# Conditioned residual block: tiles in pairs that share a matrix, norm products by seven half products

## The chip, the cores and the metric

One core of a Trainium2 chip runs the whole kernel. The metric is the device time of one execution in microseconds; 924.09 us is the median of three runs of the kernel before (919.81 to 926.35). The engines are TensorE (PE, with its weight loads shown as PEld), VectorE (DVE), ScalarE (ACT), GpSimd (POOL) and SyncE (SP, which issues DMA).

## The reference

x is 16 x 512 tokens of 512 floats. Every token has a pathway id (0 to 499), a compartment id c (0 to 4, used for cp and tm) and a flag m (0 or 1, an index into three rows of ms). All is fp32.

```python
h = _ln(x, pw_g[pathway_ids], pw_b[pathway_ids])
h = _ln(h, cp_g[compartment_ids], cp_b[compartment_ids])
t = _ln(x, tm_g[time_steps], tm_b[time_steps])          # time_steps is the same c
m = x + _mlp_ln(memory_state, ...)[:, None, :]           # n and r alike, one row per batch
s = _ln(x, ms_g[scale_type], ms_b[scale_type])           # scale_type is m
cat = concatenate([w[0]*h, w[1]*t, w[2]*m, w[3]*n, w[4]*r, w[5]*s], axis=-1)
return x + _ln(silu(cat @ int_W1 + int_b1) @ int_W2 + int_b2, int_g, int_be)
```

With xn the normalised x, `cat @ int_W1` is x times one fixed matrix (X), the twice normalised h times a fixed matrix (H), xn times a matrix that depends on the token's group (c, m) alone (V), and a row that depends on batch and group.

## The kernel before

**Head.** The 8192 tokens are sorted by their group (15 groups of c and m). Each token's place comes from running counts (`of_grp`, `run`, `pc`, `pos`). `one_hots` then makes, eight columns of tokens at a time, a one-hot of the row within a tile (`rows_`) and one of the tile (`cols_`, times the token's number): VectorE makes five or six of the eight `cols_` by a comparison and a multiplication over all of them, ScalarE the others; TensorE multiplies both into `pn`, the sorted list. Small GpSimd steps find where groups end (`place_borders`, `count_rows`, `segments`, `segment_kinds`, `segment_picks`). A tile of 128 tokens uses the matrix of the group of its middle token; tokens of another group in it get a correction from eight extra tiles, whose results go to `rows_2` in DRAM and are gathered as the row `add` (`ga`). Besides, the head computes the conditioning rows and the weights.

**Windows.** 64 tiles are worked in 16 windows of four (Q = 4). `PLACES` sets which: window w has tiles 2w and 2w+1 of the first half of the sorted order (places g = 0 and 2) and of the second half (g = 1 and 3). Per tile: gather x, statistics and norm (ScalarE), the h branch (VectorE, ScalarE, GpSimd), three turns on VectorE and DMAs on SP's queue (`spread_row`) that bring X, V and H into `cats`, the products of layer 1 in PSUM, adding of `add`, silu, a turn and DMAs into Z, layer 2, norm, output by an indirect DMA.

**Products.** X and H of a pair of tiles (2p, 2p+1) are a 2 x 2 block product done by seven half products instead of eight (`half_product`, `m7`, 4 calls of 128x256 each), with token sums on VectorE (`token_sum`, u1 to u4) and partial sums in the PSUM tiles `u` and `p1`; `half_out` (r1, r2, r3, r5) adds the parts of `u` to `add`. r1 adds the first product, while `u` holds it alone. V is done whole, four calls of 128x512 per tile (`layer1` with blk V, line 404). Its matrix is in `vs[g % 2]`, one buffer per half of the order, and is built anew only where the group changes (`s_part` on ScalarE line 257, `build` on VectorE line 265, both under `if_new`). Layer 2 is by seven too (`z_sums` on GpSimd, `seventh`, line 546), but whole in the last window (`layer2`, line 487). Window 0 uses whole products for all three blocks (lines 404).

**Order.** Every engine works its instructions in the order of the program. That order is written out by hand as names: `ORDER` (head and start), `WINDOW` (run for each w from 0 to 14, with p, c, n, m for the previous, this, the next and the window after) and `LAST`. PSUM has eight tiles of 128x512, taken in turn by `psum`.

Of the kernel before, what the change touches and what calls it, by code (L numbers as in the profile page):

```python
# [15 lines left out]
P = 128  # L16
# [10 lines left out]
    gx.e0.2 gc.0.2 fs.0.2 bd.0.1 hv.0.0 tk.1 wk.2.3 fv.0.2 gx.e0.3 cr xs.e0.1 xs.e0.2 xs.e0.3 rp.0 lX.0.1 vt.0.0
    rp.1 f2.0.2 xa.0 xe.e0 gr.e0.1 gh.0.1 fp.0.2 gx.e1.0 gx.e1.3 gx.e1.1 gx.e1.2 gr.e0.0 xp.e0 cw xm.e0 rc.0
    vv.0.1 rc.1 vv.0.3 nv.e0.1 mt.e0.1 vd.0 nv.e0.0 sp.0.0 fn.0.2 nv.e0.2 mt.e0.0 f1.0.1 lX.0.2 fs.0.1 bd.0.0
    fv.0.1 ey.1 ey.0 xs.e1.1 ro.1 ro.0 rp1 vv.0.0 xs.e1.0 xs.e1.2 ez.0 nv.e0.3 ez.1 wh gc.0.1 gr.e0.2 gx.1.2 ea.0  # L30
    lX.0.0 rp2 wl.4 xs.e1.3 f2.0.1 va.1 xs.1.2 gx.1.3 tx.1.2 xe.e1 xs.1.3 ht.0.2 ex.0 ee.0 mt.e0.2 gr.e0.3 gx.1.0
    gh.0.3 fp.0.1 lV.0.0 ey.2 eo.0 gr.e1.0 gx.1.1 xp.e1 fn.0.1 va.0 ez.2 ar mt.e0.3 hv.0.2 xa.1 tx.1.0 vd.1 xm.e1
    tx.1.3 ey.3 ht.0.1 ea.1 gc.0.3 ea.2 gh.1.3 xs.1.0 sp.0.2 ez.3 nv.e1.2 nv.e1.0 ex.1 ex.2 f1.0.3 bd.0.2 fs.0.3
    fv.0.3 mt.e1.0 ex.3 ey.4 f2.0.3 wb xs.1.1 wm.0 wm.1 wm.2 ea.3 fp.0.3 gr.e1.2 gr.e1.1 mt.e1.2 xe.1 hv.0.1 ey.6
    fn.0.3 ez.4 nv.e1.1 wm.3 nv.e1.3 ea.4 xp.1 gr.e1.3 ee.1 tx.1.1 ee.2 mt.e1.1 mt.e1.3 f1.1.3 xm.1 ee.3 eo.2 eo.1
    eo.3 ht.0.3 ey.5 ex.4 lV.0.1 ey.7 lV.0.2 ez.6 wl.2 ez.5 wl.0 ez.7 nv.1.1 nv.1.0 sp.0.3 fs.1.3 gh.1.2 sh.0.0
    gc.1.3 hv.0.3 tv.1.1 tv.1.0 bd.0.3 f1.1.2 fv.1.3 f2.1.3 ex.7 lX.0.3 lV.0.3 lH.0.2 lH.0.3 ex.6 lH.0.1 ex.5
    lH.0.0 ea.6 gc.1.2 ea.5 fp.1.3 ea.7 nv.1.3 sp.1.0 fs.1.2 fn.1.3 nv.1.2 sp.1.1 bd.1.0 tv.1.3 fv.1.2 ee.6 ee.5
    ee.4 th.1.3 f2.1.2 bd.1.1 tv.1.2 ee.7 sX.1.0 eo.4 eo.5 eo.6 eo.7 sV.1.1 sX.1.3 sV.1.0 sX.1.1 sV.1.3 sX.1.2
    sV.1.2 gc.1.0 sh.0.1 gh.1.1 fp.1.2 gh.1.0 sh.0.2 ga.0.3 sh.1.2 ga.0.1 ga.0.0 gc.1.1 ga.0.2 fn.1.2 wl.3 th.1.2  # L40
    wz f1.1.0 f1.1.1 ha.0.3 ha.0.1 ha.0.0 fs.1.0 fs.1.1 hs.0.1 hs.0.0 hs.0.3 wl.1 fv.1.0 f2.1.0 fv.1.1 tz.0.1
    tz.0.0 f2.1.1 ha.0.2 tz.0.3 sh.1.3 gx.2.0 fp.1.0 sh.1.0 gx.2.2 sh.0.3 fp.1.1 hs.0.2 fn.1.0 fn.1.1 tz.0.2 wq
    th.1.1 th.1.0 sZ.0.0 sZ.0.1 sZ.0.2 sZ.0.3 gx.2.1 gx.2.3 sH.1.3 sH.1.2 sH.1.1 sh.1.1 sH.1.0
# [28 lines left out]
    m7.c.0.4 m7.c.0.3 q7.p.1.5 q7.p.1.7 q7.p.1.1 r3.c.1 ha.c.2 ft.p.0 r3.c.0 ft.p.1 ha.c.3 ha.c.1 ha.c.0 hs.c.3
    hs.c.2 hs.c.1 hs.c.0 kf.p.2 kf.p.3 tz.c.3 tz.c.1 e0 tz.c.0 tz.c.2 sf.p.3 w2 po.p.1 sh.c.3 zs.p.7 po.p.0 sZ.c.0
    q7.p.1.6 q7.p.1.4 q7.p.1.2 q7.p.1.3 l2.c.0 ku.p.1 sl.p.2 sl.p.3 sf.p.2 yg.p.3 yg.p.2 la.c.0 lq.p.3 lq.p.2
    sd.p.3 sd.p.2 lq.c.0 sd.c.0 sZ.c.2 sZ.c.1 sZ.c.3 rv.p.2 rv.p.3 ft.p.2 rv.c.0 ft.p.3 yg.c.0 ft.c.0 l2.c.2
    l2.c.1 l2.c.3 po.p.2 po.p.3 po.c.0 la.c.2 la.c.1 lq.c.1 sd.c.1 lq.c.2 sd.c.2 rv.c.1 yg.c.1 ft.c.1 la.c.3
    yg.c.2 yg.c.3 rv.c.2 ft.c.2 e1 lq.c.3 sd.c.3 po.c.1 rv.c.3 ft.c.3 po.c.2 po.c.3
"""


@with_exitstack
def kernel(ctx: ExitStack, tc: tile.TileContext, a: dict, out: bass.AP):

# [26 lines left out]
    Q = 4  # L113
# [1435 lines left out]
```

## Time and profile before

| | us |
|---|---|
| median of 3 runs | 924.09 |
| lowest, highest | 919.81, 926.35 |
| span of the profiled execution | 920.3 |
| busy in it: PE, DVE, POOL, ACT | 884.8, 733.6, 666.9, 521.2 |

The span runs from the first to the last instruction of one profiled execution; the median lies 3.8 us above it. A group of a line is "engine operation, out<-in, shape, count | busy, mean ns of one | idle before it and what ended that". Matmuls are pipelined and their ends are modelled, so the time that a product costs in a stream is read from the start of one to the start of the next, not from its mean. Each fp32 matmul of the program is two instructions in the trace.

### The profile page before, as it was taken

To read this page: it belongs to the slowest core of one execution; us is meant where nothing else is said; L and a number is where in the kernel's file an instruction comes from. 1 tells how busy PE (TensorE), PEld (TensorE's weight loads), DVE (VectorE), ACT (ScalarE), POOL (GpSimd) and SP (SyncE) were. 2 spreads that over 40 slices of the span, in tenths; PEclk is the share of its full clock that TensorE was granted. 3 is DMA by queue.
4 is the path that set the end of the run, shared out by engine and by line. 5 is a ranking of instruction groups with operands and counts; after the bars stand their busy time and mean duration, and the time that the engine had idled before them with its cause. 6 is when DMAs were issued, how large, how long until landed. Compare 5 with 4: busy or idle time off the path is not lost.

```text
span 920.3 us, 13563 instructions
## 1 busy us (share of the span) xinstructions
PE 884.8 (96%) x3617; PEld 642.0 (70%) x3617; DVE 733.6 (80%) x1360; ACT 521.2 (57%) x1263; POOL 666.9 (72%) x730
## 2 busy tenths in 40 slices
PE   6979899999999999999999999999999999999996
PEld 6634446868677777868686877777686867778682
DVE  8776767878789798978787887869697888879565
ACT  5568736464555738374646556473657566572413
POOL 9876678576768678686878686877767676876452
PEclk9999999999999999999999999999999999999999
DMA  8755677777767777777777777777667776776513
GB/s 272 249 185 179 220 226 197 207 210 204 235 178 232 202 218 195 215 208 202 227 202 227 187 235 191 226 193 216 186 197 210 203 220 191 221 200 190 154 37 113
DMA packets 88557, 185.40 MB, mean 201 GB/s; under 512 B 24324, under 2 KB 24388, under 8 KB 88476
## 3 DMA queue, kind: packets, MB, share of 16 engines
q0 software_dynamic: 31104, 104.88, 39.4%
q1 hardware_dynamic: 56668, 79.53, 29.6%
q8 instruction: 30, 0.49, 0.2%
q14 instruction: 51, 0.42, 0.2%
q10 hardware_dynamic: 704, 0.08, 0.1%
HBM read 100.48 MB, written 19.97 MB: 131 GB/s over the span
## 4 chain that ended last, share of the span: by engine, by line
PE 50%; POOL 5%; DVE 4%; issue 3%; DMA 3%; SPq 2%; ACT 1%; POOLq 0%; DVEq 0%; ACTq 0%
PE u L452 13%; PE p L404 13%; PE p L452 11%; PE pq_0b L546 4%; PE pq_1b L546 4%; PE pq_1a L546 3%; PE pq_0a L546 2%; SPq L205 2%; DMA catZ<-rZ 2%; POOL xbs L391 1%; POOL out L638 1%; DMA pw<-in_pw,i_pw 1%; DVE vs L265 1%; DVE yb L634 0%; DVE yb L633 0%
## 5 line engine op out<-in xcount | busy, mean ns | idle before, releaser
L404 PE MATMUL p<-vs,catV 128*128 128x512 f32 x512 | 228.3, 593 | 3.9 <-DVE vs L265 1.7
L404 PEld LDWEIGHTS p<-vs,catV 128*128 128x128 f32 x512 | 96.9, 190 | 108.5 <-issue 99.6
L452 PE MATMUL p<-wh__81,catH 128*128 128x256 f32 x480 | 111.0, 379 | 0.0
L452 PEld LDWEIGHTS p<-wh__81,catH 128*128 128x128 f32 x480 | 91.4, 190 | 12.2
L376 ACT ACTIVATE pw<-pw,rsh 128x512 f32<-128x512 f32 x64 | 45.6, 714 | 95.2 <-DVE pw L383 76.9
L638 POOL DMA_INDIRECT out<-yb,tok x64 | 75.4, 1178 | 31.2 <-issue 15.1
L475 ACT ACTIVATE add<-add 128x512 f32<-128x512 f32 x64 | 39.7, 625 | 94.4 <-DVE add L472 93.1
L350 ACT ACTIVATE junk<-pw 128x512 bf16<-128x512 f32 x60 | 37.5, 626 | 85.8 <-DVE pw L347 78.1
L171 POOL DMA_INDIRECT cp<-cp_rows,i_cp x64 | 73.4, 1147 | 15.5 <-issue 13.2
L391 POOL TENSOR_TENSOR xbs<-xbs,rows 128x512 f32<-128x512 f32 x64 | 82.4, 1289 | 1.4
L171 POOL DMA_INDIRECT pw<-in_pw,i_pw x64 | 63.0, 984 | 28.1 <-DVE rH L197 13.0
L625 POOL TENSOR_TENSOR rsy<-vey,mhalf 128x4 f32<-128x4 f32 (+1 forms) x16 | 23.6, 1473 | 82.3 <-DVE veh L368 69.5
L171 POOL DMA_INDIRECT xbs<-in_x,tok x64 | 65.1, 1017 | 19.9 <-issue 18.1
L171 POOL DMA_INDIRECT add<-rows,i_add x64 | 67.0, 1048 | 16.6 <-issue 16.5
L383 DVE SCALAR_TENSOR_TENSOR pw<-pw,sumsh,cp 128x512 f32<-128x512 f32 x60 | 45.5, 760 | 32.9 <-DMA cp<-cp_rows,i_cp 32.8
L317 ACT ACTIVATE xm<-xbs,nmx,rsx 128x512 f32<-128x512 f32 x64 | 48.8, 806 | 22.9 <-DVE nmx L311 17.2
L372 POOL TENSOR_TENSOR rsh<-veh,mhalf 128x1 f32<-128x1 f32 x64 | 48.6, 760 | 13.0 <-DVE veh L368 11.5
L347 DVE SCALAR_TENSOR_TENSOR pw<-pw,rsx 128x512 f32<-128x512 f32 x64 | 56.0, 876 | 2.3
L452 PE MATMUL p<-wt,catH 128*128 128x256 f32 x240 | 56.7, 379 | 0.0
L452 PE MATMUL u<-wt,catX 128*128 128x256 f32 x240 | 56.5, 379 | 0.0
L452 PEld LDWEIGHTS u<-wx__80,catX 128*128 128x128 f32 x240 | 45.7, 190 | 12.6 <-issue 3.8
L452 PE MATMUL u<-wt,ss 128*128 128x256 f32 x240 | 54.4, 379 | 0.0
(439 smaller groups left out, 2127.7 us busy)
## 6 DMA issues: line engine op xcount, KB each, us to landing
catX<-rX SPq DMA_DIRECT2D x240, 64.0 KB
catV<-rV SPq DMA_DIRECT2D x240, 64.0 KB
catZ<-rZ SPq DMA_DIRECT2D x240, 64.0 KB
catH<-rH SPq DMA_DIRECT2D x240, 64.0 KB
rows<-adde SPq DMA_DIRECT2D x8, 256.0 KB
yb<-in_int_W SPq DMA_DIRECT2D x1, 1024.0 KB
catH<-in_int_W SPq DMA_DIRECT2D x1, 1024.0 KB
w1x<-in_int_W SPq DMA_DIRECT2D x1, 1024.0 KB
```

Of the source, the lines that this page charges most:

```text
L171: nc.gpsimd.indirect_dma_start(dst, None, table, bass.IndirectOffsetOnAxis(ap=idx, axis=0), **kw)
L317: nc.scalar.activation(t, st["xb"][:, j, :], AF.Identity, bias=st["nm"][:, j : j + 1], scale=st["rs"][:, j : j + 1])
L347: nc.vector.scalar_tensor_tensor(h, h, st["rs"][:, j : j + 1], pw[:, D:], ALU.mult, ALU.add)
L372: nc.gpsimd.tensor_tensor(rs, st.pop(("ve", j)), mhalf[:, :1], ALU.pow)
L376: nc.scalar.mul(pw[:, :D], pw[:, :D], st.pop(("rs", j)))
L383: nc.vector.scalar_tensor_tensor(pw[:, :D], pw[:, :D], st["sh", j][:, 1], cp, ALU.add, ALU.mult)
L391: nc.gpsimd.tensor_add(st["xb"][:, j, :], st["xb"][:, j, :], rows[:, 2, :])
L404: nc.tensor.matmul(st["p1", g], st["c" + blk][:, g, c, :], m[:, c, :], start=(blk == first and c == order[0]), stop=(blk == last and c == ...
L452: nc.tensor.matmul(dst, m[:, c], at_["half1"][k][:, c], start=(k == 1 and c == 0), stop=(c == NC - 1), skip_group_check=True)
L475: nc.scalar.activation(st["add", g], st["add", g], AF.Silu)
L546: nc.tensor.matmul(st["pq", 2 * p + i][:, half], st["zp", p][k][:, c], at_["half"][k][:, c], start=False, stop=(c == 1), skip_group_check= ...
L638: nc.gpsimd.indirect_dma_start(out_rows[j], bass.IndirectOffsetOnAxis(ap=tok[:, j, w : w + 1], axis=0), yb[:, j, :], None)
```

## The change

Tiles are put in another order: `i_q`, the place of each tile, is now computed from the counts (a few small products on TensorE in front of the sort). First come pairs of tiles of the same group, then the tiles left over; 50 places (`2 * PURE`) are always filled by such pairs. For these, V is done by seven half products too (`norm_product`, v7, 2 calls of 128x256 each), added in PSUM onto the seven of X and H. Its sums of token blocks are on VectorE (`norm_sum`, yv, four per pair), its differences of matrix blocks are made once per build and fill `vs[1]`; `vs[0]` holds the matrix. The last 14 places use whole products (`whole_product`, lW) with `vs[0]` and `vs[1]` in turn. The first product and the sum of the first and seventh are copied by ScalarE from `u` into both halves of a tile's `p1` (`copy_first`, cf), and r1 goes away. The fifth product then overwrites that half of `u`.

In the sort, each of six columns of `cols_` is made by one operation with two scalars, and ScalarE makes two of eight. The places of tile borders (`i_pos` and others) are computed by GpSimd from `i_q`; `segments`, `segment_kinds` and `segment_picks` stand behind the first gathers; the sorted list goes to DRAM by an indirect DMA of GpSimd instead of one of SP. `ORDER` is new and goes on until window 1, `WINDOW` is new and runs for windows 2 to 11, `LAST` lists windows 12 to 15 name by name.

```diff
 def if_new(st, g, engine, part):
-        if st["w"] == 0 and g < 2:
+        if tile_of(st, g) in (0, 2 * PURE + 1):
             part()
 def build(st, g):
-        w, v = st["w"], v_of(st, g)
+        if one_matrix(st, g) and g % 2:
+            return
+        w, v = st["w"], vs[g % 2]
...
                 nc.vector.scalar_tensor_tensor(v[:, c], wt[:, c], sct[:, c, g, w : w + 1], v[:, c], ALU.mult, ALU.add)
+            if one_matrix(st, g):
+                nc.vector.tensor_sub(v_half(5), b12, b11)
+                nc.vector.tensor_sub(v_half(7), b22, b12)
+                nc.vector.tensor_sub(v_half(6), b22, v_half(5))
+                nc.vector.tensor_sub(v_half(4), b21, v_half(6))
+    def norm_sum(st, p, k):
...
+            st["sv"] = catp.tile([P, 2, 4, 2, P], F32, tag="rotV", name=f"sv{st['w']}")
+        s1, s2, s3, s4 = [st["sv"][:, p, n] for n in range(4)]
         if k == 1:
             nc.vector.tensor_add(s1, a21, a22)
...
+    def home_of(st, p, k):
+        key, half = {1: ("u", 0), 7: ("u", 0), 5: ("u", 0), 6: ("u", 1), 2: ("a", 0), 3: ("a", 1), 4: ("b", 0)}[k]
...
+    def norm_product(st, p, k):
...
+        for c in range(2):
+            nc.tensor.matmul(dst, m[:, c], v_half(k)[:, c], start=(k == 5 and c == 0), stop=(c == 1),
+                             skip_group_check=True)
+    def whole_product(st, g):
...
+        for c in range(NC):
+            nc.tensor.matmul(st["p1", g], st["cV"][:, g, c, :], vs[g % 2][:, c, :], start=False, stop=(c == NC - 1),
+                             skip_group_check=True)
+    def copy_first(st, g):
...
+        nc.scalar.copy(st["p1", g].rearrange("p (k n) -> p k n", k=2),
+                       st["u", g // 2][:, :H].unsqueeze(1).to_broadcast([P, 2, H]))
     def half_out(st, kind, p):
...
-        if kind == "1":
-            nc.vector.tensor_add(a[:, :H], a[:, :H], u)
...
-        m = U - 3 + (k % 3 == 2 or k == NQ // U - 1)
+        m = U - 2
...
-        nc.vector.tensor_tensor(cols_[:, :m], i_q.unsqueeze(1).to_broadcast([P, m, NQ]),
-                                pcol[:, q0 : q0 + m].unsqueeze(2).to_broadcast([P, m, NQ]), ALU.is_equal)
-        nc.vector.tensor_tensor(cols_[:, :m], cols_[:, :m],
-                                vals[:, q0 : q0 + m].unsqueeze(2).to_broadcast([P, m, NQ]), ALU.mult)
+        for u in range(m):
+            nc.vector.tensor_scalar(cols_[:, u], i_q, pcol[:, q0 + u : q0 + u + 1], vals[:, q0 + u : q0 + u + 1],
+                                    ALU.is_equal, ALU.mult)
...
+    for k, (m, v) in enumerate(((ones[:1], i_q[:1]), (ones[:NG], in_pairs), (ones[:NG], single))):
+        nc.tensor.matmul(pto[:, NQ : 2 * NQ], m, v, start=(k == 0), stop=(k == 2))
+    cond_1(1)
+    nc.scalar.copy(i_q, pto[:, NQ : 2 * NQ])
...
-    nc.sync.dma_start(in_order.rearrange("(k r) o -> k (r o)", r=P), at_c)
...
     gather_x(w0)
+    nc.gpsimd.indirect_dma_start(in_order.rearrange("(k r) o -> k (r o)", r=P),
+                                 bass.IndirectOffsetOnAxis(ap=i_tile, axis=0), at_c, None)
     tile_pairs_out(*tile_pairs())
     row_pairs_out(*row_pairs())
+    segments()
+    segment_kinds()
+    segment_picks()
+    segment_ends()
...
-    for w in range(NW - 1):
+    for w in range(2, 12):
         run(WINDOW, w)
-    run(LAST, NW - 1)
+    run(LAST)
```

A part of the new `WINDOW`, for the order around the copies (m7, v7 and q7 on TensorE, cf, sp, f and kf on ScalarE or VectorE):

```
 m7.c.0.1 v7.c.0.1 cf.c.0 gh.c.3 m7.c.1.1 sh.p.2 tz.p.1 xs.n.3 tz.p.2 v7.c.0.2 sh.p.0
 sZ.p.0 m7.c.0.7 yv.c.0.1 yv.c.0.3 ga.c.1 yv.c.0.2 xs.n.2 v7.c.0.7 ga.c.3 po.o.0 lb.o.1 gx.n.1 yv.c.0.4 v7.c.0.3
 sp.c.2 cf.c.1 f1.c.2 v7.c.0.5 v7.c.0.6 f1.c.3 po.o.1 sZ.p.1 va.n v7.c.0.4 bd.c.2 v7.c.1.1 fs.c.2 fv.c.2 q7.p.0.2
```

## Rows read from the trace of the kernel before

**Rows 1.** The page: busy us (share of span) and instructions of each engine.

```profile
PE 884.8 (96%) x3617; PEld 642.0 (70%) x3617; DVE 733.6 (80%) x1360; ACT 521.2 (57%) x1263; POOL 666.9 (72%) x730
```

**Rows 2.** Chain of waits in time: start us, us, what; one window, then six later.

```profile
313.20 3.43 PE p L404 x8
...
321.82 6.91 PE u L452 x32
...
339.08 6.87 PE p L404 x16
...
613.49 2.59 PE p L404 x6
```

**Rows 3.** Groups by line: norm products, r1, a 128x256 sum, builds, a copy into PSUM.

```profile
L404 PE MATMUL p<-vs,catV 128*128 128x512 f32 x512 | 228.3, 593 | 3.9 <-DVE vs L265 1.7 <-ACTq L248 1.4 <-PEq L1374 0.6
...
L265 DVE SCALAR_TENSOR_TENSOR vs<-wt,sct,vs 128x512 f32<-128x512 f32 x44 | 30.2, 748 | 1.5 <-ACT vs L257 1.5
...
L257 ACT ACTIVATE vs<-ws,scs 128x512 f32<-128x512 f32 x44 | 28.1, 710 | 1.8 <-PE p L404 1.5 <-ACTq L248 0.2
...
L574 DVE TENSOR_TENSOR yb<-yb 128x256 f32<-128x256 f32 x30 | 15.9, 530 | 2.7 <-ACT yb L569 2.7
...
L461 DVE TENSOR_TENSOR add<-add,u 128x256 f32<-128x256 f32 x30 | 12.1, 403 | 19.8 <-DMA add<-rows,i_add 17.8 <-PE p L404 1.9
...
L520 ACT COPY pq_0a<-rows 128x512 f32<-128x512 f32 x15 | 8.7, 579 | 0.0
```

**Rows 4.** Stretches of 50 us: busy PE, PEld, DVE, ACT, POOL; clock, DMA share, GB/s.

```profile
320.00:370.00 50.00, 50.00 (x202) 38.08 (x201) 45.95 (x82) 31.45 (x75) 38.71 (x38) 1.00 0.74 211
...
470.00:520.00 50.00, 50.00 (x202) 38.08 (x201) 40.57 (x73) 28.45 (x71) 38.20 (x38) 1.00 0.75 210
...
770.00:820.00 50.00, 49.40 (x199) 37.34 (x198) 42.02 (x76) 29.81 (x72) 37.39 (x39) 1.00 0.72 210
```

**Rows 5.** Timeline of TensorE: start us, us, line, out<-in, count, [idle before, releaser].

```profile
69.08 3.60 PE L404 MATMUL p<-wx__80,catX 128*128 128x512 f32 x8
...
93.66 10.46 PE L1376 MATMUL pe<-wt,catZ 128*128 128x512 f32 x24
...
142.93 3.62 PE L452 MATMUL u<-wx__80,catX 128*128 128x256 f32 x16
...
161.55 3.60 PE L404 MATMUL p<-vs,catV 128*128 128x512 f32 x8
...
644.53 3.67 PE L404 MATMUL p<-vs,catV 128*128 128x512 f32 x8 [1.73 <-DVE vs L265]
...
820.20 3.60 PE L404 MATMUL p<-vs,catV 128*128 128x512 f32 x8
...
897.46 13.97 PE L487 MATMUL p<-w,catV 128*128 128x512 f32 x32
```

**Rows 6.** Timeline of VectorE in the sort.

```profile
12.70 0.20 DVE L855 TENSOR_SCALAR rc<-pi 128x64 int32<-128x64 int32 x1
12.81 0.19 DVE L856 TENSOR_SCALAR rc<-pi 128x64 int32<-128x64 int32 x1
...
13.35 1.23 DVE L883 TENSOR_TENSOR vs<-catZ 128x1024 f32<-128x1024 f32 x1
...
14.49 0.48 DVE L885 TENSOR_TENSOR vs<-room,catZ 128x320 f32<-128x320 f32 x1
```

**Rows 7.** Timeline of GpSimd, a small step beside the sort and one after it.

```profile
22.72 1.63 POOL L938 TENSOR_SCALAR side<-bf 14x1 f32<-14x1 f32 x1
...
31.91 0.23 POOL L971 TENSOR_SCALAR m<-grp 14x2 f32<-14x2 f32 x1
```

**Rows 8.** Timeline of all engines within a steady window.

```profile
492.00 0.75 DVE L347 SCALAR_TENSOR_TENSOR pw<-pw,rsx 128x512 f32<-128x512 f32 x1
...
495.13 2.07 DVE L347 SCALAR_TENSOR_TENSOR pw<-pw,rsx 128x512 f32<-128x512 f32 x1
495.37 1.28 POOL L391 TENSOR_TENSOR xbs<-xbs,rows 128x512 f32<-128x512 f32 x1
```

More of the change, by code (lines that the diff above doesn't have):

```diff
@@ L27 @@
[L27 to L36, printed above, removed]
@@ L260, in build @@
     def build(st, g):
-        w, v = st["w"], v_of(st, g)
+        if one_matrix(st, g) and g % 2:
+            return
+        w, v = st["w"], vs[g % 2]
+        H = D // 2
+        b11, b12, b21, b22 = [v[:, 2 * r : 2 * r + 2, k * H : (k + 1) * H] for r in range(2) for k in range(2)]
         def part():
@@ L404, in layer1 @@
             nc.tensor.matmul(st["p1", g], st["c" + blk][:, g, c, :], m[:, c, :],
-                             start=(blk == first and c == order[0]), stop=(blk == last and c == order[-1]),
-                             skip_group_check=st["w"] > 0)
+                             start=(blk == first and c == order[0]), stop=(blk == last and c == order[-1]))
     def awake(kind, at, n):
@@ new lines @@
+    n_odd, n_end, n_up, n_left, n_less = [prep.tile([P, 1], F32, name=n)[:NG]
+                                          for n in ("n_odd", "n_end", "n_up", "n_left", "n_less")]
+    in_pairs, single = [prep.tile([P, NQ], F32, name=n)[:NG] for n in ("in_pairs", "single")]
+    pto = psum("pto")
+    cond_1(0, range(1))
+    nc.tensor.matmul(pto[:NG, :1], t_in[:NQ], by_turns[:NQ], start=True, stop=True)
+    nc.tensor.matmul(pto[:NG, 1:2], t_ends[:NQ, 1:], ones[:NQ, :1], start=True, stop=True)
+    nc.scalar.activation(n_odd, pto[:NG, :1], AF.Square)
@@ new lines @@
+    nc.scalar.copy(n_end, pto[:NG, 1:2])
+    cond_1(0, range(1, 2))
+    nc.tensor.matmul(pto[:NG, 2:3], below[:NG, :NG], n_odd, start=True, stop=True)
+    nc.tensor.matmul(pto[:NG, 3:4], above[:NG, :NG], n_odd, start=True, stop=True)
+    nc.scalar.activation(n_up, pto[:NG, 2:3], AF.Identity, scale=-1.0, bias=n_end)
+    nc.scalar.copy(n_left, pto[:NG, 3:4])
+    nc.vector.tensor_scalar(in_pairs, i_slot[:NG], n_up, n_odd, ALU.is_ge, ALU.mult)
+    nc.vector.tensor_scalar(n_less, n_up, -1.0 - NQ, n_odd, ALU.add, ALU.mult)
@@ new lines @@
+    nc.vector.tensor_scalar(single, i_back[:NG], n_left, n_less, ALU.is_equal, ALU.mult)
+    cond_1(0, range(2, NC))
+    cond_1(2)
+    for k, (m, v) in enumerate(((ones[:1], i_q[:1]), (ones[:NG], in_pairs), (ones[:NG], single))):
+        nc.tensor.matmul(pto[:, NQ : 2 * NQ], m, v, start=(k == 0), stop=(k == 2))
+    cond_1(1)
+    nc.scalar.copy(i_q, pto[:, NQ : 2 * NQ])
+    nc.tensor.matmul(pto[:NQ, 4:5], i_q[:1], ones[:1, :1], start=True, stop=True)
+    i_tile = prep.tile([P, 1], I32, name="i_tile")[:NQ]
@@ L833 @@
+    nc.scalar.copy(i_tile, pto[:NQ, 4:5])
     spare = rows.rearrange("p v f -> p (v f)")[:NB]
```

294 lines of the change are left out of this document (206 added, 88 removed).

## The prediction

> **What bounds the kernel now.** I read the page first, then the chain of waits, the groups by line, the stretches of 50 us, and last the timelines of single engines. The page gives TensorE 96% of the span, VectorE 80%, GpSimd 72% and ScalarE 57% [rows 1]. A busy share alone proves little, so the chain comes next. In the middle of the kernel it is TensorE and nothing else, one product after another, and the same item returns at 313.20 and at 613.49, six windows later: 300.29/6 = 50.05 us per window [rows 2]. The same can be built from prices. 16 instructions of 128x512 take 6.87 us, 0.4292 each; 32 of 128x256 take 6.91, 0.2159 each [rows 2] (each call of the code is two instructions: the group of the norm products counts 512 where the 64 tiles have 4 calls each [rows 3]). A window has 32 of 512 columns for the norm products V, 112 of 256 for the products of X and H, and 56 of 256 for layer 2: 13.74 + 24.18 + 12.09 = 50.01. So a steady window has no idle TensorE time, at a granted clock of 1.00 [rows 4], and time goes down only if TensorE gets less to do, as long as the others follow. VectorE is the nearest: 40.57 of 50 us in a stretch without a build of a matrix, 45.95 in one with two, both without loss on TensorE; GpSimd has 38.2, ScalarE 28.5 [rows 4].
>
> Outside the steady windows: the first real product starts at 69.08, and the products of layer 2's last window at 897.46 run for 13.97; the same item of windows 1 and 14 starts at 161.55 and 820.20 [rows 5], 658.65 us for 13 windows, which is 8.3 more than 13 x 50.03. One example of these stalls is the 1.73 us at 644.53 behind a freshly built matrix [rows 5].
>
> **The change part by part.** *The norm products by seven.* For each pair that shares its matrix, 2 x 4 calls of 512 columns (16 instructions, 6.87 us) become 7 x 2 calls of 256 columns (28 instructions x 0.2159 = 6.04 us): 0.82 us less [rows 2]. The first 50 places are such pairs by construction; window 0 keeps its whole products, so places 4 to 49 count: 23 pairs, 18.9 us, and a steady window falls to 48.39 us. This is work taken from the engine that sets the end, so nothing has to be hidden for it to count.
>
> *VectorE.* Per window with two such pairs eight sums of 128x256 are new (a comparable one has a mean of 0.53, with 0.40 for the addition of the partial sum that goes, twice per window [rows 3]): +4.2 - 0.8 = +3.4 us, so 44.0 of 48.39 are busy and 4.4 are left. They are hidden behind TensorE; without that cover they would cost those 3.4 us a window. Four windows (2, 5, 7 and 10) also get a new matrix for pairs: four products at 0.75 [rows 3] and four differences of as many elements, about 6 us: 50, more than the window. The work evens out over two windows, as 45.95 did; I charge 0.5 us each, 2 in all, between 0 and the whole excess of 4 x 1.6 = 6.
>
> *ScalarE.* 60 copies of 128x512 (four per window from 1 on) at 0.58 [rows 3] are new, 2.3 us a window: 30.8 of 48.4. The place matters more than the sum. The second copy of a pair reads M1+M7 before the fifth product overwrites it, and TensorE has only the third product in between, 4 x 0.2159 = 0.86 us. 0.58 fits if ScalarE is free then. What stands ahead of the copy in its queue (a build of the next matrix, a row's sums) delays it, and behind it TensorE's whole queue. No row shows this wait: below nothing it can't be, above it is two activations of 0.71 [rows 3] ahead of it, 2 x 0.71 + 0.58 - 0.86 = 1.14 us for each of 23 pairs. With a free engine half of the time or more I take 0.04 per pair, 1 us.
>
> *More builds.* The reference's inputs fill only 10 of 15 groups: five with 1366 to 1467 tokens, five with 187 to 225. By the token in the middle of each tile these have 11, 11, 11, 11, 12, 1, 2, 2, 2 and 1 tiles. In the old order that makes 11 builds (44 instructions [rows 3]), five of them from window 12 on. In the new order there are 18: at places 0, 10, 20, 30, 40, then at 51 and at every place from 52 to 63, since the last 14 places have two buffers that hold a different group each time. From place 51 on each costs 4 x 0.71 on ScalarE and 4 x 0.75 on VectorE [rows 3]. The stretch 770 to 820 holds 42.0 us of VectorE with one build [rows 4]; three more at 3.0, without the 0.8, make 50.2 of 50. So window 13 has no slack, the later ones have, since nothing follows that they prepare. Of the old builds one showed 1.73 [rows 5], most nothing. I take 0.25 for each of the 8 added at the end: 2 us, between 0 and 8 x 1.73 = 14.
>
> *The sort.* A round of eight columns had one comparison of rows (1.14 us to the next start) and two operations of 320 columns at about 0.5 each [rows 6]; now six small two-scalar operations. Two independent ones of 128x64 started 0.11 us apart [rows 6]: 0.66 against 1.04, 8 rounds, 3 us less; at the 0.20 that one lasts it is 1.2 against 1.04, 1.3 us more. The places now depend on the counts, so in front of the first round come two small comparisons, a start of the long additions that waits for the counts, three more small operations and a chain VectorE, TensorE, ScalarE, twice: about 2 us later. Net -1 us, between -3 and +3.3.
>
> *Moved steps.* The segment steps (21 GpSimd instructions) go behind the first gathers. Beside VectorE's sort such an instruction took 1.63 us, after it 0.23 [rows 7], so they cost 21 x 0.29 = 6 us there, and an indirect store is new: whatever hangs on them, the token lists, then the eight extra tiles (now from 93.66 [rows 5]), comes about 7 us later. The new list puts more of window 0 ahead: after the last extra product 48 instructions of 512 columns remain, 20.6 us, where before 80 did (34 of the 39 us to window 1's first product at 142.93 [rows 5]). The 14 us moved ahead cover 7. I charge nothing; uncovered it is 7 us.
>
> Sum: -18.9 - 1 + 2 + 1 + 2 = -14.9. The new lists also can win back some of the 8.3 us of stalls; I take 1 of them: -15.9. Against the profiled execution's span of 920.3 that is 904.4. The median of the runs is 924.1, 3.8 above that span, so I forecast 924.1 - 15.9 = 908 us, and 903 to 913 for this case.
>
> One row speaks against VectorE's reserve. At 495.13 a scaled addition on VectorE took 2.07 us where the same one took 0.75 at 492.00; GpSimd's addition of 1.28 us started 0.24 after it [rows 8]. So the two engines hold each other up at times, here for 1.3 us, once in that window for certain. The Trainium skill ("SBUF — State Buffer", section "Who interferes with whom") says that a VectorE instruction with two inputs in SBUF and a GpSimd instruction that reads SBUF exclude each other; by it each of the eight new sums could meet one. The trace agrees in that row, and shows no such loss for most others. What it would make of the time is the second rival.
>
> **The rivals.** *The lists win more* (chance 0.12): the stalls of 8.3 us go and the head shortens by 3: 908 - 11 = 897. For it: head and tail are listed anew and windows 12 to 15 one by one, with their builds; against: the last windows are fuller than before.
>
> *VectorE takes over as the bound* (0.13): if three of the eight sums per window lose 1.3 us each, the 4.4 us are used up and half of the saving is lost: 908 + 9 = 917. For it [rows 8] and 40.6 busy already; against: 45.95 without loss.
>
> *The last builds come through* (0.08): 13 builds from place 51 on, each with the 1.73 us of 644.53: 22 us less the 2 charged is more than the saving, 928; at 1 us each 919. For it: each place waits for ScalarE, then VectorE; against: two buffers and some 12 us of other products per tile.
>
> *The extras come too late* (0.06): 908 + 7 = 915.
>
> *The copies hold TensorE* (0.06; the other side): at 1.14 us per pair 26 us, 908 - 1 + 26 = 933. Slower than before from 0.7 us per pair on. For it: ScalarE is in order and has a build's branch ahead of that copy in the list; against: it is idle 17 us a window.
>
> That the change does nothing can be left out: the products are in the program whatever the data.
>
> **How the numbers follow.** My forecast has 0.55. About 1% is what a measurement of this kernel can tell from no change, 914.8 to 933.3. Faster: 0.52 of the forecast, 0.12, and of the three rivals near the border 0.05 + 0.02 + 0.03 = 0.74. Same: 0.03 + 0.08 + 0.06 + 0.03 = 0.20. Slower: 0.06, the copies alone. The range 897 to 919 holds the forecast, half of the better lists and most of the three nearer rivals, about 0.8.
>
> **What would show it.** Right: the same item of the chain returns every 48.4 to 49 us; the norm products count 28 instructions of 256 columns per pair; VectorE at 43 to 45 per window; no more than 0.1 us ahead of the fifth product. The copies would show as TensorE idle just before the fifth product, released by ScalarE; VectorE as bound by a chain of VectorE through a steady window and a period near 50; the builds as idle ahead of the whole products of windows 13 to 15; the extras as a gap between 100 and 150 us. The forecast is wrong if a steady window stays at 50, or if the last four windows take more than 210 us.

## The result, and the profile after

The changed kernel takes 931.85 us (median of 5 runs, 931.24 to 936.29) beside 920.82 for the kernel before (5 runs, 919.05 to 926.35): 1.012 times, with a 95% interval of 1.0084 to 1.0155. It is slower by 1.2%, where 908 was forecast. (The forecast of 908 started from 924.1, the median of three runs; with more runs the kernel before stands between 920.8 and 922.5, so differences are compared below.) Run again, the same kernel stood at 933.1 beside 922.4 on one chip (ratio 1.0100, 1.0054 to 1.0147) and at 924.4 beside 922.5 on another (1.0039, 1.0014 to 1.0064). That difference is a part of the story.

The page of the changed kernel, in the columns of [rows 1]; its span is 934.5 us, 14.2 more than the 920.3 of before:

```profile
PE 878.3 (94%) x3909; PEld 698.6 (75%) x3909; DVE 780.1 (83%) x1512; ACT 570.2 (61%) x1347; POOL 664.1 (71%) x735
```

TensorE has less to do, 878.3 us against 884.8, and yet a longer span: it waits more. Stretches of 50 us, in the columns of [rows 4]:

```profile
270.00:320.00 50.00, 50.00 (x233) 43.89 (x232) 42.89 (x83) 31.61 (x76) 39.34 (x40) 1.00 0.76 221
...
350.00:400.00 50.00, 48.14 (x220) 41.27 (x220) 45.51 (x83) 32.10 (x79) 40.13 (x41) 1.00 0.74 215
450.00:500.00 50.00, 48.52 (x225) 42.06 (x224) 47.10 (x88) 33.16 (x78) 38.31 (x39) 1.00 0.72 207
```

In the first, without a build, TensorE is busy throughout, as before, with 42.89 us of VectorE beside it. The other two hold the builds of windows 5 and 7: VectorE 45.51 and 47.10, and TensorE loses 1.9 and 1.5 us. The groups by line that answer to [rows 3]: norm products of pairs, of single tiles, VectorE's part of a build, the copies.

```profile
L565 PE MATMUL u<-vs,sv 128*128 128x256 f32 x276 | 69.4, 389 | 2.9 <-ACT vs L325 1.5 <-ACT p L580 1.5
...
L572 PE MATMUL p<-vs,catV 128*128 128x512 f32 x112 | 51.7, 612 | 3.5 <-DVE vs L337 2.8 <-ACT p L580 0.7
L337 DVE SCALAR_TENSOR_TENSOR vs<-wt,sct,vs 128x512 f32<-128x512 f32 x72 | 51.5, 772 | 1.5 <-ACT vs L325 1.1 <-issue 0.2
...
L565 PE MATMUL p<-vs,catV 128*128 128x256 f32 x184 | 46.0, 381 | 7.0 <-ACT p L580 4.0 <-issue 3.1
...
L580 ACT COPY p<-u 128x512 f32<-128x512 f32 x60 | 34.1, 570 | 40.9 <-PE u L565 16.4 <-issue 11.9 <-remote 6.2
```

Nearly all the new idle time of TensorE among the norm products stands behind ScalarE (the copies L580, its part of a build, L325) and behind a matrix just built (L337); 3.1 us have no releaser in the profile ("issue").

Where the time went can be counted from TensorE's timeline. The first product of a window is one and the same item in every window, so the differences of its starts are the windows' lengths; what is over the matmuls in it at 0.4292 and 0.2159 us [rows 2] is lost time. A window without loss has 224 instructions of 128x256, 48.36 us.

| length of window, us | 2 | 3 | 4 | 5 | 6 | 7 | 8 | 9 | 10 | 11 |
|---|---|---|---|---|---|---|---|---|---|---|
| before | 49.99 | 50.95 | 50.55 | 49.99 | 50.16 | 50.00 | 49.99 | 50.15 | 51.96 | 51.53 |
| changed, first profile | 53.56 | 48.41 | 49.75 | 51.17 | 48.42 | 50.24 | 48.41 | 49.45 | 51.24 | 48.41 |
| changed, another chip (e9) | 51.31 | 48.42 | 49.44 | 49.25 | 48.42 | 50.25 | 48.41 | 49.45 | 49.26 | 48.41 |
| e3, no builds for pairs | 48.41 | 48.41 | 48.41 | 48.41 | 48.41 | 48.41 | 48.41 | 48.41 | 48.41 | 48.41 |

Against the profile of before, in us, with the forecast's terms beside it (its 1 for the copies and its 1 won back are in the third line; e9, e10 and e13 are described below; each number is rounded by itself):

| | forecast | changed | e9 | e10 | e13 |
|---|---|---|---|---|---|
| start of the first product | -1 | +11.4 | +10.5 | +3.1 | +3.0 |
| lost in windows 0 and 1 | 0 | +1.7 | +2.5 | +1.7 | +4.1 |
| lost in windows 2 to 11 | +2 | +10.2 | +3.8 | +4.1 | -4.7 |
| lost in windows 12 to 15 | +2 | +9.1 | +3.5 | +5.0 | -1.2 |
| matmuls from first product to last layer 2 | -18.9 | -19.8 | -19.8 | -19.8 | -19.8 |
| from the last layer 2 to the end | 0 | +1.7 | +1.7 | +1.7 | +1.7 |
| sum (span less that of before) | -15.9 | +14.3 | +2.2 | -4.2 | -17.0 |

So the saving came in full, and it was eaten at three places above all: the head, the windows around builds, and the last four. The 1.7 to 4.1 us of windows 0 and 1 stay unexplained. In the last stretch ScalarE loads a table for 1.28 us at 921.84, ahead of the roots that the last outputs wait for, where the kernel before makes its last such load at 899.80; whether that is the 1.7 us was not tested.

**The head.** TensorE's timeline up to the first product [rows 5 has 69.08 for it], and GpSimd's beside it:

```profile
54.14 0.21 PE L1172 MATMUL pst<-of_seg,room 14*14 14x4 f32 x2 [6.07 <-DVE stx L234]
...
57.70 3.14 PE L1297 MATMUL pnx<-steps,room 14*128 14x4 f32 x14 [2.54 <-POOL room L1176]
60.77 1.92 PE L1364 MATMUL pdr<-tg,picks 8*34 8x512 f32 x2
...
80.48 1.88 PE L481 MATMUL p<-wx__80,catX 128*128 128x512 f32 x4
```

```profile
27.42 0.18 POOL L1110 TENSOR_TENSOR n_b<-nn 14x1 f32<-14x1 f32 x1
39.82 1.23 POOL L229 DMA_INDIRECT xbs<-in_x,tok  x1 [12.22 <-PE ptp L1181]
...
46.11 0.18 POOL L1126 TENSOR_TENSOR of_s<-begs,bf 14x1 f32<-14x1 f32 x1
...
51.70 0.18 POOL L1154 TENSOR_TENSOR of_seg<-t,c 14x1 f32<-14x1 f32 x1
...
53.91 0.18 POOL L1165 TENSOR_TENSOR of_seg<-t 14x1 f32<-14x1 f32 x1
```

GpSimd has nothing to do for 12.2 us during the sort, then issues the gathers, and only then works the segment steps, 46.11 to 51.88. The small product `pst` waits for their end, and behind it in TensorE's queue stand products of the conditioning (`pdr`, `hs`), which read nothing of the steps; behind the steps in GpSimd's queue stand the next gathers. The releaser named, a sum of VectorE (L234), only ends at the same moment: `pst` reads `of_seg`, which GpSimd finishes at 54.09.

VectorE's queue is held by the same steps, a little earlier. Its `segment_ends` (L1157, L1158) reads what they make, and behind it stand the operands of the conditioning: `sel` for `hs`, and `picks` for `pdr`.

```profile
49.30 0.15 DVE L1157 TENSOR_TENSOR of_seg<-m 14x1 f32<-14x1 f32 x1 [9.04 <-POOL m L1141]
51.91 0.15 DVE L1158 TENSOR_TENSOR t<-m 14x1 f32<-14x1 f32 x1 [2.46 <-POOL of_seg L1154]
...
56.95 0.73 DVE L1356 TENSOR_SCALAR picks<-picks,i_row 8x34 f32<-8x34 f32 x1 [0.58 <-issue]
```

So `pdr` and `hs` could not have run at 48 even with `pst` behind them; no experiment parts the two holds.

The sort itself, in VectorE's timeline (compare [rows 6]):

```profile
15.38 1.22 DVE L1051 TENSOR_TENSOR vs<-catZ 128x1024 f32<-128x1024 f32 x1
16.52 1.49 DVE L1054 TENSOR_SCALAR vs<-room,catZ 128x64 f32<-128x64 f32 x6
```

It starts 2.0 us later (15.38 against 13.35), and its six column operations take 1.49 us (1.40 to the next start), where the two before took 0.93 from 14.49 to the next start.

### The profile page after: what moved, and what is told of

Read it like the earlier page. It is cut to its first block, busy times and chain, and to the rows that moved or that the text cites. A ratio compares the mean times of both kernels' runs of the same rounds, so it can differ in the third digit from the quotient of the medians.

```text
span 934.5 us, 14604 instructions
## 1 busy us (share of the span) xinstructions
PE 878.3 (94%) x3909; PEld 698.6 (75%) x3909; DVE 780.1 (83%) x1512; ACT 570.2 (61%) x1347; POOL 664.1 (71%) x735
## 5 line engine op out<-in xcount | busy, mean ns | idle before, releaser
L449 POOL TENSOR_TENSOR rsh<-veh,mhalf 128x1 f32<-128x1 f32 x64 | 54.0, 845 | 55.8 <-DVE veh L445 53.5
L229 POOL DMA_INDIRECT cp<-cp_rows,i_cp x64 | 68.8, 1075 | 18.5 <-issue 8.9
L229 POOL DMA_INDIRECT pw<-in_pw,i_pw x64 | 66.7, 1042 | 18.0 <-issue 9.2
L565 PE MATMUL u<-vs,sv 128*128 128x256 f32 x276 | 69.4, 389 | 2.9 <-ACT vs L325 1.5
L565 PEld LDWEIGHTS u<-vs,sv 128*128 128x128 f32 x276 | 52.3, 193 | 12.5 <-ACT p L580 2.1
L598 DVE TENSOR_TENSOR add<-p,add 128x512 f32<-128x512 f32 x64 | 43.1, 679 | 20.2 <-PE p L553 15.6
L580 ACT COPY p<-u 128x512 f32<-128x512 f32 x60 | 34.1, 570 | 40.9 <-PE u L565 16.4
L553 PE MATMUL u<-wx__80,ss 128*128 128x256 f32 x240 | 56.9, 381 | 1.1 <-DVE ss L514 0.9
L553 PE MATMUL u<-wx__80,catX 128*128 128x256 f32 x240 | 56.7, 380 | 0.0
L572 PE MATMUL p<-vs,catV 128*128 128x512 f32 x112 | 51.7, 612 | 3.5 <-DVE vs L337 2.8
```

The source lines that it names most:

```text
L229: nc.gpsimd.indirect_dma_start(dst, None, table, bass.IndirectOffsetOnAxis(ap=idx, axis=0), **kw)
L449: nc.gpsimd.tensor_tensor(rs, st.pop(("ve", j)), mhalf[:, :1], ALU.pow)
L553: nc.tensor.matmul(dst, m[:, c], at_["half1"][k][:, c], start=(k in (1, 1 if one_matrix(st, a) else 5) and c == 0), stop=(c == NC - 1), sk ...
L565: nc.tensor.matmul(dst, m[:, c], v_half(k)[:, c], start=(k == 5 and c == 0), stop=(c == 1), skip_group_check=True)
L572: nc.tensor.matmul(st["p1", g], st["cV"][:, g, c, :], vs[g % 2][:, c, :], start=False, stop=(c == NC - 1), skip_group_check=True)
L580: nc.scalar.copy(st["p1", g].rearrange("p (k n) -> p k n", k=2), st["u", g // 2][:, :H].unsqueeze(1).to_broadcast([P, 2, H]))
```

## The experiments

Where an edit undoes a part, "+" is what the experiment has and "-" what the changed kernel has. e1 to e4 ran on one chip, e5 to e8 on a second, e9 to e12 on a third, e13 to e15 on the first again. Each set has its own runs of the kernel before: 921.7, 922.4, 922.5 and 921.2 us.

**e1: the segment steps back in the sort.**

```
-        for make in {0: (first_rows, count_rows, place_borders), 3: (count_ends,)}...
+        for make in {0: (first_rows, count_rows, place_borders), 3: (count_ends, segments, segment_kinds)}...
     row_places()
+    segment_picks()
...
     row_pairs_out(*row_pairs())
-    segments()
-    segment_kinds()
-    segment_picks()
     segment_ends()
```

> The changed kernel with one part undone: the segment steps (segments, segment_kinds) are back in the fourth round of the sort and segment_picks right behind row_places, where GpSimd of the changed kernel is idle from 27.6 to 39.8 us. Theory: behind the first gathers these steps hold the small product pst and with it TensorE's whole queue (6.07 us idle ahead of pst, 2.54 ahead of pnx), so the first product of layer 1 comes back from 80.5 to about 73 us and the whole kernel gains 6 to 8: 924 to 926 against 932 for the changed kernel. Rival (the prediction's own step): the 14 us of window 0's work put ahead cover the delay, so the first product may come earlier but the end stays: 931 to 932.

916.2 us, ratio 0.9934 (0.9915 to 0.9953): the first product starts at 71.97. But the time fell by 15.6 and not by 7, and so it went with the next three.

**e2: the columns by two operations again** (the lines of the diff for `cols_`, reversed).

> The changed kernel with one part undone: the columns of the sort are made by two operations over all of them as before. Theory: six small two-scalar operations take 1.4 to 1.5 us a round in the changed trace instead of about 1.0, and a round is 2.47 us instead of about 2.2, so going back ends the sort 2 to 3 us earlier and gives 929 to 930 against 932. Rival 1 (the prediction's value): the small operations are the cheaper ones, going back costs 3 us: 935. Rival 2: the sort's end is not on the path, since the loads of the weights and the conditioning rows come later: 932.

921.1 us, ratio 0.9995 (0.9971 to 1.0019), 10.8 less than the changed kernel; the first product moved by 2.4 only, to 78.09 (by 1.4 against e3 and e4 of the same chip, 79.5).

**e3: no builds for pairs.**

```
     def if_new(st, g, engine, part):
+        if one_matrix(st, g) and tile_of(st, g):
+            return
```

> The changed kernel without the four new matrices of the pairs in windows 2, 5, 7 and 10 (their ScalarE and VectorE parts and the differences are left out; places 4 to 49 go on with the first matrix, so their result is another). Theory: the losses of TensorE around these windows (5.3 us more than before in window 2, 3.8 in 4 and 5, 2.0 in 7, 2 in 9 and 10) are the builds', and all windows 2 to 11 fall to 48.4: 919 to 923 against 932. Rival (the prediction's step): a build window costs 0.5, so this gains 2: 930. Second rival: window 2 loses to something else (late DMAs after the start), then 4 to 7 are gained and window 2 stays near 53.

915.2 us, ratio 0.9922 (0.9894 to 0.9949). Every window from 2 to 11 has 48.41 us (table above), so none of them loses more than 0.05 to the copies or to VectorE when no matrix is made.

**e4: no builds at the last twelve places** (`if tile_of(st, g) > 2 * PURE + 1: return` at the same place).

> The changed kernel without the builds of the last twelve places (52 to 63; their ScalarE and VectorE parts are left out, these tiles use the matrices that stand there, so their result is another). Theory: TensorE loses 14 us in windows 12 to 15 where it lost 5 before, and these 9 us are the builds': 922 to 924 against 932. Rival (the prediction's step, 0.25 us per added build): 930. Second rival: the loss of window 12 (3.0 us ahead of a norm product, with nothing built there) is not a build's and stays: 926.

920.1 us, ratio 0.9976 (0.9953 to 0.9998). Windows 12 to 15 lose 4.6 us.

All four lay 11 to 17 us below 931.9, whatever they undid, and none showed the 3.0 us ahead of a norm product in window 2, nor the one in window 12. The changed kernel itself had to be run again.

**e5: the changed kernel again.**

> The changed kernel as it is, once more, beside the others. Each of e1 to e4 came out 11 to 17 us under the changed kernel's 931.9, also where only 2 us hang on the part that was undone (e2: 921.1). Theory 1: some 9 us of losses (3.0 in window 2, 1.9 in 5, 1.0 in 10, 5.2 in 12) belong to the one occasion on which the changed kernel was run, not to the kernel: 922 to 926 here, with window 2 near 51 and window 12 near 48. Theory 2: they are the kernel's own, from a timing that any edit moves: 930 to 933 again.

933.1 us, ratio 1.0100 (1.0054 to 1.0147), with both waits in its profile: theory 2, as it seemed.

**e6: e1 and e2 together.**

> The changed kernel with e1's and e2's edits together: the segment steps back in the sort, the columns by two operations over all. Theory: both lie on the head's path one behind the other (first product 72.0 with the first edit, 78.1 instead of 80.5 with the second), so it starts near 69.5 and the time is e1's less 2.4: 913 to 915. Rival: after the steps have gone forward the sort's end waits for other work (weights, conditioning rows), and the time stays at e1's 916.

926.2 us, ratio 1.0046 (1.0023 to 1.0068): more than e1 or e2 alone. Neither expectation holds; the first product is at 72.91, but the waits of windows 2 and 12 are back.

**e7: the copy ahead of the build's part.**

```
-    sp.c.2 cf.c.1 f1.c.2 v7.c.0.5 v7.c.0.6
+    cf.c.1 sp.c.2 f1.c.2 v7.c.0.5 v7.c.0.6
```

> e6 with one name moved in the list of windows: the second copy of the first pair stands ahead of ScalarE's part of a new matrix (cf.c.1 sp.c.2 in place of sp.c.2 cf.c.1). Theory (the prediction's mechanism for the copies, in the build windows alone): in windows 2 and 7 TensorE waits 1.5 us for this copy behind the four activations of a build; moved ahead, the 1.5 us and the 0.6 behind them go in both: 3 to 4 us less than e6, 909 to 911. Rival: the matrix itself is late, so the same wait comes back ahead of the first product that needs it: as e6, 913 to 915.

928.0 us, ratio 1.0047 (1.0026 to 1.0067), no gain on e6. In window 7 the second copy is no longer waited for, but the four activations of the build, with the row statistics behind them, now stand ahead of the third one, and TensorE waits there:

```profile
454.77 1.89 PE L672 MATMUL pq_0a<-w,catZ 128*128 128x256 f32 x8
458.59 1.73 PE L553 MATMUL u<-wt,catX 128*128 128x256 f32 x6 [1.94 <-ACT p L580]
```

The rival was right in kind: the wait only changed its place.

**e8: the kernel before with the six column operations alone** (the diff for `cols_`, in the kernel before).

> The kernel before with one part of the change alone: six columns of eight in the sort by one two-scalar operation each, two by ScalarE. Theory: six such operations take 1.4 to 1.5 us where the two over all took about 1.0, 8 rounds: 2 to 3 us more than before, 923.5 to 925 against 921.7. Rival 1 (the prediction's value, 0.11 us each): 3 us less, 918.7. Rival 2: not on the path: 921.7.

925.0 us, ratio 1.0035 (1.0010 to 1.0060), in line with the theory; the last product of the sort starts at 33.03 instead of 31.32. But its first product of layer 1, at 68.61, is not later than before (69.08); its span is 2.5 us longer by windows, not by the head. So it isn't shown that the 2.6 us come from the sort.

**e9: the changed kernel on a third chip.**

> The changed kernel as it is, beside e10 to e12. In its first two profiles ScalarE's copy at the start of window 2 and one in window 12 begin 2.6 to 3.4 us after the products that they read, and TensorE waits behind them; e6 and e7, on the chip of e5, show the same, e1 to e4, on another chip, show none of it although lists and work are the same there. Theory: this part (about 8 us, with the clock at half after it) hangs on the chip. Then this is 931 to 934 if both stalls are in its profile, and 922 to 925 if neither is. Rival: the kernel's own, and e1 to e4 lost it by their edits: 931 to 934 with the stalls while e10 has none.

924.4 us, ratio 1.0039 (1.0014 to 1.0064), without the two waits. **e10: e1's kernel beside it.**

> e1's kernel once more, beside the changed kernel itself. Theory: whatever the chip adds is the same for both, so the two differ by what the segment steps cost in the head, 7 to 9 us (first product 72 against 80.5): 914 to 917 if e9 has no stalls in windows 2 and 12, 923 to 926 if it has them. Rival: the edit takes the stalls away too: 916 beside an e9 of 932.

916.7 us, ratio 0.9941 (0.9925 to 0.9958), 7.8 less than e9. Here the same four points of TensorE's queue stand at

```profile
48.43 0.20 PE L1172 MATMUL pst<-of_seg,room 14*14 14x4 f32 x2
...
51.46 2.12 PE L1295 MATMUL pnx<-steps,room 14*128 14x4 f32 x14 [2.28 <-POOL room L1176]
53.51 1.92 PE L1362 MATMUL pdr<-tg,picks 8*34 8x512 f32 x2
72.21 7.03 PE L481 MATMUL p<-wx__80,catX 128*128 128x512 f32 x16
```

so the segment steps are worth 7.35 us at the first product (79.56 in e9) and as much at the end: 5.8 at `pst` (54.24 in e9), 0.5 more in the wait for `room`, 1.0 more in `pnx`, and nothing behind `pdr`, from whose start to the first product e9 and e10 take 18.69 and 18.70.

**e11 and e12: two gathers later in windows 2 and 12**, in the changed kernel and in e10's.

```
+        if w == 2:
+            names = names.replace(" ga.c.1 ", " ").replace(" ga.c.3 ", " ").replace(" cf.c.2 ", " cf.c.2 ga.c.1 ga.c.3 ")
...
-    hs.11.0 tz.11.2 gh.12.2 ga.12.1 ga.12.3 m7.11.0.4 ...
+    hs.11.0 tz.11.2 gh.12.2 m7.11.0.4 ... v7.12.0.7 cf.12.1 ga.12.1 ga.12.3
```

> The changed kernel with two gathers of the rows to be added (ga for tiles 1 and 3) put later in windows 2 and 12 alone, behind a copy. In the stretches of the two stalls GpSimd issues eight indirect DMAs one behind the other and the gathers move 280 to 360 KB a microsecond, in the windows between 140 to 260. Theory: the late copies hang on this burst, so on a chip that shows the stalls they shrink or go: 3 to 8 us less than e9. Rival: the burst is by chance at the same place: as e9 within 2.

> e10's and e11's edits together. Theory (both pay): 914 to 917 on either kind of chip, faster than the kernel before by 0.5 to 0.9%. Rival (the burst does not matter): as e10 within 2.

926.2 and 919.6 us, 1.7 and 3.0 more than e9 and e10. As this chip has no late copies, the edit was not put to the test; it costs a little by itself. The burst alone can't be the cause, though: in e9 DMA moves 324 GB/s at 199.5 to 205.5, as in e5 at the late copy (325 at 200 to 206), and nothing waits.

**e13: e10's kernel without any later build.** **e14: e6's kernel once more. e15: e10's once more.**

> e10's kernel without any build behind the first matrix of either kind (the four for pairs and the twelve of places 52 to 63 are left out, so the result of these tiles is another). Closing the account. Theory: head and builds are all that went wrong, and they add: e10's 916.6 less 9.4 us (the losses of windows 2, 4, 5, 7, 9 and 10 in its profile) less 3 to 5 (windows 12 to 15): 902 to 905, which is what the prediction asked for (its 908 less the 4 us that it charged to builds). Rival: the builds cover other stalls that come out then (copies, sums of VectorE): above 908.

> e6's kernel once more, beside e15 (the same without the edit of the columns). The last product of the sort ends 1.5 us earlier with the two operations over all columns (e2 and e6 against the changed kernel). Theory: with the segment steps forward it is off the path, and the two are equal within 1.5 us. Rival: it is on the path, 1.5 to 2.5 us less than e15. Should this chip show the late copies of windows 2 and 12, both stand near 925, otherwise near 916.

> e10's kernel, beside e13 and e14: 915 to 918 on a chip without the late copies of windows 2 and 12, 923 to 926 with them. If the chip shows them for e14 and not here, they hang on the edit of the columns and not on the chip.

904.8 us (ratio 0.9819, 0.9788 to 0.9850), 914.6 (0.9918, 0.9896 to 0.9941) and 915.3 (0.9944, 0.9923 to 0.9965). e13's 904.8 is the forecast's 908 less its 4 for builds, but partly by luck: it gains 16.4 on its own kernel before (921.2), where the forecast without builds asks for 19.9, and its head is still 3.0 late. e14 and e15 can't be told apart (0.7 us), so no cost of the columns is shown once the steps have gone forward; the rival fell. And e14 is e6, kernel for kernel: 926.2 us on the second chip, 914.6 on the first. The start of window 2 on ScalarE and TensorE, e6:

```profile
192.70 1.13 ACT L601 ACTIVATE add<-add 128x512 f32<-128x512 f32 x2
197.21 0.57 ACT L580 COPY p<-u 128x512 f32<-128x512 f32 x1 [3.37 <-remote]
```

```profile
192.93 1.89 PE L553 MATMUL u<-wx__80,catX 128*128 128x256 f32 x8
197.83 2.07 PE L565 MATMUL p<-vs,catV 128*128 128x256 f32 x4 [3.02 <-issue]
```

and e14:

```profile
192.24 1.13 ACT L601 ACTIVATE add<-add 128x512 f32<-128x512 f32 x2
193.28 0.57 ACT L580 COPY p<-u 128x512 f32<-128x512 f32 x1
```

```profile
191.25 1.89 PE L553 MATMUL u<-wx__80,catX 128*128 128x256 f32 x8
193.91 1.13 PE L565 MATMUL p<-vs,catV 128*128 128x256 f32 x4 [0.76 <-ACT p L580]
```

In e14 the copy follows at once on the activations ahead of it. In e6 ScalarE is as free, the products that the copy reads were issued before 192.93, and it begins 3.37 us late; TensorE's next product needs the copy. The copy itself waits for TensorE's semaphore alone. The last of the products that step it ends at 193.09, and the trace has the semaphore stepped at 192.91, 195.04 and 197.19, the last just before the copy starts; in e14 the steps are recorded where the products end (the last at 191.43). The first profile, e5 and e7 show the same, 3.8 to 4.2 us in window 2 and 2.7 to 3.3 in window 12. So, as far as the records go, it is TensorE's release that comes late, not ScalarE. In e6 the clock then stands at half for 3.4 us, and window 2 has 55.18 us there against 52.50 in e14.

e14's kernel (on the first chip) and e10's (on the first and the third) beat both kernels of this case, by 0.6 to 0.8% of the kernel before; on the second chip e14's kernel (e6) was slower than before.

## Why the prediction was wrong, point by point

**The norm products: right.** A window without a build has 48.41 us in the profiles of the table (forecast 48.39), and the matmuls fell by 19.8 us: the 18.9, and 0.9 for two instructions of 512 columns that stood behind the first product and now stand ahead of it.

**VectorE as the bound: right to be put second.** Windows 3, 6, 8 and 11 run without loss at 42.89 us of VectorE in 50, and the new sums have means of 0.40 to 0.42 us, one kind 0.58, where 0.53 was taken. But the collision of [rows 8] does come back in some profiles. In the first, three of the 92 sums take 0.82, 2.16 and 2.66 us, in windows 5 and 10, with an addition of GpSimd beside the two slowest:

```profile
368.89 2.16 DVE L527 TENSOR_TENSOR sv<-catV 128x256 f32<-128x256 f32 x1
```

```profile
369.51 1.25 POOL L468 TENSOR_TENSOR xbs<-xbs,rows 128x512 f32<-128x512 f32 x1
```

Behind them TensorE waits for VectorE, and these two windows have 51.17 and 51.24 us there, 1.9 and 2.0 more than in e9, where no sum is slow. Part of that is a late copy that comes before. e6 shows the same three; e5, e7, e9 and e10 none. The rule of the Trainium skill that the prediction weighed ("SBUF — State Buffer", section "Who interferes with whom") shows in these three sums; none of the other 89 takes over 0.6 us.

**The builds of pairs: the term was mis-sized**, 0.5 us for each of four windows with a bound of 6 for all, from VectorE's excess over the window. e3 against e9 gives 9.3 us (two chips). In e9 windows 2, 4, 5, 7, 9 and 10 are 8.5 over 48.41 together, and on one chip e1 and e2 lose 9.3 more than e3 in windows 2 to 11. The excess of VectorE was the smaller part: of TensorE's waits in these windows of e9 3.9 us stand behind ScalarE's copies and 1.0 behind a token sum of VectorE; 0.9 have no releaser. e9, window 7, ScalarE and TensorE:

```profile
451.56 1.32 ACT L325 ACTIVATE vs<-ws,scs 128x512 f32<-128x512 f32 x2
453.15 1.33 ACT L325 ACTIVATE vs<-ws,scs 128x512 f32<-128x512 f32 x2 [0.27 <-PE p L565]
454.39 0.58 ACT L580 COPY p<-u 128x512 f32<-128x512 f32 x1
```

```profile
452.51 1.03 PE L565 MATMUL p<-vs,sv 128*128 128x256 f32 x4
455.02 2.00 PE L565 MATMUL u<-vs,sv 128*128 128x256 f32 x8 [1.48 <-ACT p L580]
```

Four activations of a build stand ahead of the second copy, and TensorE's fifth product stands behind that copy. The prediction had this very order in its rival of the copies, with a price of two activations and for every pair; it comes in windows 2 and 7 only, where it is four. In windows 5 and 10 the first copy is late by 0.48, and the windows before them lose 0.52 ahead of a product of H behind its token sum on VectorE. e7 shows that the four activations can't simply be put elsewhere in that stretch.

**The copies otherwise: right** (next to nothing with ScalarE free, as e3's windows show; forecast 1 us for all).

**The last builds: mis-sized by half.** Forecast 2 us, and 4.4 by e4 against e9 (two chips; windows 12 to 15 lose 8.3 in e9 and 4.6 in e4). On e4's own chip e1, e2 and e3 lose 7.8 to 8.2 there, which makes it 3.1 to 3.5; one kernel has 9.8, 6.3 and 7.8 there (e10, e15, e1), so the size is not exact. e9, window 15, where the matrix of the first tile comes too late:

```profile
848.22 2.55 ACT L325 ACTIVATE vs<-ws,scs 128x512 f32<-128x512 f32 x4
...
853.37 3.28 ACT L325 ACTIVATE vs<-ws,scs 128x512 f32<-128x512 f32 x4
```

```profile
851.34 2.72 DVE L337 SCALAR_TENSOR_TENSOR vs<-wt,sct,vs 128x512 f32<-128x512 f32 x4
```

```profile
852.22 10.54 PE L572 MATMUL p<-vs,catV 128*128 128x512 f32 x24 [2.12 <-DVE vs L337]
```

All sixteen builds together are 10.5 us by e13 against e15, one chip.

**The sort: the sign was wrong.** A small two-scalar operation costs 0.23 to 0.25 us in a row of six (1.41 to 1.49), not the 0.11 at which two others of [rows 6] started, and not the 0.20 of the upper bound. The start was 2.0 us late, as forecast. The end is 3.7 us late (34.99 against 31.32 for the last round's products) where -1 was charged and 3.3 was the upper bound (the lower one, -3, leaves out the late start). What of it reaches the end of the kernel is not pinned down: e2 is 3.4 below e9 (two chips), e8 2.6 above its kernel before but not by its head, and e14 0.7 below e15, within the spread.

**The moved steps: the step that failed.** The prediction saw the delay, about 7 us, and looked for it at the token lists and the extra tiles, behind which 14 us of other work lie; so it charged nothing. It asked what the steps compute, not what stands behind their first readers: `pst` is in TensorE's queue ahead of the conditioning and of the first product, and `segment_ends` is in VectorE's queue ahead of `sel` and `picks`, and none of them needs the steps. It is 7.8 us by e10 against e9, of which 7.35 are there at the first product. That the steps cause it is shown; which of the two queues would bind alone is not. A small part of it is the clock. After the wait TensorE's granted clock is half,

```profile
52.00:66.00 14.00, 9.10 (x36) 5.51 (x40) 10.76 (x40) 3.58 (x11) 10.23 (x15) 0.50 0.20 61
```

so at 1.2 GHz the 14 small products of `pnx` take 3.14 us and `pdr` 1.92, where in the profile of before, at full clock, they take 1.70 and 1.04:

```profile
48.09 1.70 PE L1127 MATMUL pnx<-steps,room 14*128 14x4 f32 x14
...
51.28 1.04 PE L1194 MATMUL pdr<-tg,picks 8*34 8x512 f32 x2
```

e10 falls to half as well, later and for 6.8 us instead of 17.1 (`pnx` 2.12, `pdr` 1.92), so the moved steps answer for 1.0 us of this.

**The stalls won back: more than charged.** 1 us was taken. Without builds (e3, e13) windows 2 to 11 lose 4.7 us less than before. About 1.9 of that is the wait for a matrix at 644.53 [rows 5], a build of the kernel before that has no counterpart there; the other 2.8 are waits in layer 2 that the new order does not have. The builds took more than that back.

**Not foreseen at all: the late copies.** 931.9 and 933.1 against 924.4 for one kernel: 8 us that come and go with the occasion; with e6 and e14 it is 11.6. No row of before could show them, since the kernel before has no such copies.

Without these, the forecast of 908 would still have missed: e9's 924.4 is outside its 897 to 919. Of the 18 us between e9's +2.2 and the forecast's -15.9, 11.5 are the start of the first product, 4.3 windows 0 to 11 (2.5 and 1.8), 1.5 the last windows, 1.7 the end, less 0.9 of matmuls. The copies' rival (933) has the measured time by luck and not the mechanism: it took a wait at every pair. The extras' rival (915) had the right cause and the wrong victim.

## What to carry to other kernels

Before a step is moved, list not only what reads its result but what stands behind each reader in its engine's queue: here 6 us of small GpSimd steps held the queues of TensorE and of VectorE. In a stream that runs without slack, rare events cost by their place in a queue (four activations ahead of a copy), not by the average load of their engine. And when every undone part gains more than it can be worth, run the changed kernel itself again beside it before a cause is named.

## What the runs showed of the hardware

The same kernel took 8 to 12 us more on one chip than on another (e5 and e9, e6 and e14), without a difference in the kernel before (921.7, 922.4 and 922.5 us). The place is the same each time: a copy of ScalarE in window 2 (3.36 us late in e5, 3.37 in e6) and one in window 12, with TensorE idle behind them 3.10 and 2.58 us in e5, and often the clock at half after that. In the profiles that show it about a third of the semaphore events is missing (16,353 recorded in the changed kernel's first profile, 25,038 in e9's); e8, a variant of the kernel before on the second chip, lacks as many and has no such wait. In all four the semaphore of TensorE that the copy waits for is recorded as stepped 2.7 to 4.2 us after the products end, just before the copy starts. Why stays open, the chip and its records included: the one experiment on it (e11) met a chip without late copies, and the burst of gathers at these places is as strong in e9, which has none.
